# Attention kernel, one core: three quarters of the row exponentials kept instead of half, exchanged within and not across the two partition halves, V times them in 64x32 tiles, and all exchange DMAs on one queue

## Chip, cores and metric

One Trainium2 chip, one core of it. The metric is the device time of one execution in microseconds (us), lower is better. The kernel before has a median of 650.43 us over three runs (650.21 to 651.04).

## What is computed

The input x is 8 batches of 512 tokens by 512 features, all float32. Queries, keys and values are projections of x with biases; a condition vector of each batch is projected with the same Wq and Wk and added to queries and keys. Then come attention with 16 heads of 32 features and a residual.

```python
cQ = split_heads(x @ Wq.T + bq) + split_heads(cond @ Wq.T + bq)
cK = split_heads(x @ Wk.T + bk) + split_heads(cond @ Wk.T + bk)
V = split_heads(x @ Wv.T + bv)
attn = softmax(einsum("bhqd,bhkd->bhqk", cQ, cK) / sqrt(32))
out = x + merge_heads(einsum("bhqk,bhkd->bhqd", attn, V))
```

## The kernel before

The work is cut into T = 32 groups t, each of one batch (b = t // 4) and four heads. A group has 512 query rows, worked in four blocks of 128 (qc). For each block and each head j:

- **Row scores** (row_scores, L641): a 32x128 weight tile against 512 keys. The four heads sit on four bands of 32 partitions, so that four such matmuls fill the array, each into a PSUM bank of its own.
- **Row maxima** on VectorE (one_max L593, row_max_of L650), then the **row exponential** on ScalarE with the sum of each row (denominators, L701).
- These exponentials lie with queries on the partitions, while V needs keys there. For half of the query blocks (KQ = 2 of NS = 4) they are **kept** in SBUF: VectorE turns them in 32x32 squares (turn_kept, L660, four instructions of 1024 columns a group), and DMAs exchange the off-diagonal blocks between the four bands of 32 partitions (swap_kept, L682). Six pairs of blocks, three moves each (a block to the side, its partner into its place, the side into the partner's): 18 DMAs of 128 KB a group, some issued by SP and some by GpSimd. For the other half, **the rest**, scores are made a second time with keys on the partitions (less_max L772 subtracts the maxima, scores_of_rest L785), and eight exponentials go through ScalarE again (rest_leaves, L799).
- **V** (times_v_half, L840): weight tiles of 128 partitions by 32 columns, four side by side, 32 matmuls of 256 columns for each group. Row sums (spread_sums L875) and a reciprocal (L885) follow; VectorE turns the result back (L912), GpSimd scales it and adds the residual (L913, L914), and SP stores it with four DMAs (L917).

The **projections** of the next batch run in between. Each is a Strassen-like scheme: an item is "first" or "other" of q, k or v for a half u; MADE lists them, three a group. Their matmuls (product, L462) are 128x32 tiles again. What combines the products is shared by VectorE (L487, L531, L555, L1236, L1238), ScalarE copies and GpSimd additions. x comes in 32-row bands by four DMAs a block (L172), is turned by VectorE (L372), and comes again as the residual (L190).

The order on every engine is written out by hand (manual_schedule): an engine takes its instructions in the order of the code, and waits for semaphores in that order. This holds for the DMA queues of SP and GpSimd too. The loop runs thirds(t) for t = 1 to 28, one group each; below it is called a step. Step t multiplies V for group t-1, makes the rest of group t, and the row scores and maxima of groups t+1 and t+2. A first part makes weights, condition and group 0; a last part does groups 29 to 31.

In a step TensorE switches six times between the two tile shapes: 32x128 for scores, 128x32 for V and projections. A stretch of one shape is called a burst.

## Time and profile before

| what | us |
|---|---|
| median of three runs | 650.43 |
| span of the profiled execution, first to last instruction | 648.4 |
| TensorE (PE) busy | 641.6 |
| VectorE (DVE) busy | 600.1 |
| ScalarE (ACT) busy | 533.9 |
| GpSimd (POOL) busy | 410.6 |

The profiled execution has no time of its own beside its span; the median of the runs stands 2.0 us above the span. The page gives busy time by engine and by group of instructions; the timeline shows instructions in order of time, runs of the same kind merged into one row; a row's numbers are its start and its length in us, and the length ends with the last instruction's end, so that the distance to the next row's start says better what a row costs. Matmuls come in the trace as two records each, weight loads as well. The waits view sums who waited for whom.

### The profile page before, as it was taken

The numbers are of one execution on the slowest core, as the hardware profiler recorded it, in microseconds if no ns is written. First come the engines' busy times: TensorE is split into PE (matmuls) and PEld (weight loads), VectorE is DVE, ScalarE is ACT, GpSimd is POOL, SyncE is SP. The second block draws the span as 40 slices with busy tenths as digits, with TensorE's granted clock in tenths as the row PEclk, the third lists the DMA queues.
The fourth block names the chain that finished last, engine by engine and source line by source line (L and its number), as shares of the span: only waits on it lengthen the run. The fifth ranks groups of instructions, "written<-read, shape, count | busy, mean of one in ns | idle before, by whom it ended". The sixth has DMA issues, their size and how long they took to land. (4 is left out here: it accounts for less than half of the span.)

```text
span 648.4 us, 24814 instructions
## 1 busy us (share of the span) xinstructions
PE 641.6 (99%) x9856; PEld 356.7 (55%) x9856; DVE 600.1 (93%) x845; ACT 533.9 (82%) x1364; POOL 410.6 (63%) x651
## 2 busy tenths in 40 slices
PE   9999999999999999999999999999999999999997
PEld 8445555556555555555555555555555555555531
DVE  3799999999999999999999999999999999999887
ACT  2479888889888989888888988898988888898564
POOL 3633655686665776758567776558766576665650
PEclk9999999999999999999999999999999999999999
DMA  7615688878888788977888978788888767797921
GB/s 191 107 27 84 131 164 172 168 169 191 168 171 174 158 182 177 200 156 153 181 178 170 201 154 186 161 175 169 179 193 162 153 144 164 153 188 155 199 48 34
DMA packets 248457, 102.02 MB, mean 157 GB/s; under 512 B 229962, under 2 KB 230474, under 8 KB 248340
## 3 DMA queue, kind: packets, MB, share of 16 engines
q1 hardware_dynamic: 234196, 65.54, 53.6%
q0 software_dynamic: 12384, 33.83, 20.2%
q8 instruction: 78, 1.28, 0.8%
q10 hardware_dynamic: 1760, 1.05, 0.5%
q14 instruction: 39, 0.32, 0.1%
HBM read 19.75 MB, written 8.39 MB: 43 GB/s over the span
## 5 line engine op out<-in xcount | busy, mean ns | idle before, releaser
L593 DVE TENSOR_REDUCE nmax<-psum 128x1 f32<-128x512 f32 x279 | 177.5, 675 | 9.3 <-PE psum L641 4.9
L701 ACT ACTIVATE psum<-psum,nmax 128x512 f32<-128x512 f32 x248 | 165.3, 678 | 3.6 <-DVE nmax L593 3.0
L641 PE MATMUL psum<-kT,qT 32*128 32x512 f32 x1024 | 162.0, 612 | 0.0
L701 ACT ACTIVATE store<-psum,nmax 128x512 f32<-128x512 f32 x204 | 139.6, 701 | 24.9 <-DVE nmax L593 24.7
L682 POOL DMA_DIRECT2D store<-store x258 | 129.0, 504 | 48.9 <-DMA store<-store 31.8
L799 ACT ACTIVATE store<-psum 128x512 f32<-128x512 f32 x232 | 119.8, 602 | 33.2 <-PE psum L785 33.2
L660 DVE STREAM_TRANSPOSE store<-store 128x1024 f32<-128x1024 f32 x116 | 138.9, 1217 | 0.0
L650 DVE TENSOR_REDUCE nmax<-psum 128x2 f32<-128x1024 f32 x98 | 118.8, 1212 | 0.0
L840 PE MATMUL psum<-store,v 128*32 128x256 f32 x1856 | 106.8, 381 | 0.9 <-DMA store<-store 0.9
L840 PEld LDWEIGHTS psum<-store,v 128*32 128x32 f32 x1856 | 57.2, 110 | 57.9 <-ACT wT_q L632 21.2
L913 POOL TENSOR_TENSOR res<-res,recs 128x512 f32<-128x512 f32 x30 | 31.4, 1046 | 89.0 <-DVE res L912 89.0
L785 PE MATMUL psum<-qT,kT 32*128 32x256 f32 x928 | 83.8, 374 | 0.0
L641 PEld LDWEIGHTS psum<-kT,qT 32*128 32x128 f32 x1024 | 61.5, 183 | 35.4 <-issue 17.8
L785 PEld LDWEIGHTS psum<-qT,kT 32*128 32x128 f32 x928 | 60.8, 184 | 5.9 <-issue 0.3
L701 ACT ACTIVATION_READ_ACCUMULATOR psum<-psum,nmax 128x1 f32 x248 | 55.0, 222 | 0.0
L203 POOL TENSOR_TENSOR xr<-xr,bvs 128x512 f32<-128x512 f32 x30 | 38.6, 1285 | 16.4 <-DMA xr<-in_x_dram 15.7
L462 PE MATMUL psum<-wc_v,xc 128*32 128x256 f32 x768 | 47.7, 379 | 0.0
L462 PE MATMUL psum<-xc,wc_q 128*32 128x256 f32 x720 | 44.7, 379 | 0.0
L462 PE MATMUL psum<-xc,wc_k 128*32 128x256 f32 x720 | 44.5, 379 | 0.0
L701 ACT ACTIVATION_READ_ACCUMULATOR store<-psum,nmax 128x1 f32 x204 | 44.3, 217 | 0.0
L914 POOL TENSOR_TENSOR res<-res,xr 128x512 f32<-128x512 f32 x30 | 38.3, 1278 | 2.3
L462 PE MATMUL psum<-xT,wT_k 128*32 128x256 f32 x480 | 34.5, 382 | 0.0
(191 smaller groups left out, 972.4 us busy)
## 6 DMA issues: line engine op xcount, KB each, us to landing
store<-store SPq DMA_DIRECT2D x264, 128.0 KB, 2.7
store<-store POOLq DMA_DIRECT2D x258, 128.0 KB, 3.8
out_dram<-res SPq DMA_DIRECT2D x122, 64.0 KB, 3.7
xr<-in_x_dram SPq DMA_DIRECT2D x120, 64.0 KB, 4.2
x<-in_x_dram SPq DMA_DIRECT2D x112, 64.0 KB, 3.3
w_q<-in_L_cond_Wq_dram SPq DMA_DIRECT2D x4, 256.0 KB, 3.9
w_v<-in_L_cond_Wv_dram SPq DMA_DIRECT2D x16, 64.0 KB, 2.5
w_k<-in_L_cond_Wk_dram SPq DMA_DIRECT2D x16, 48.0 KB, 2.7
```

The source lines that it names most:

```text
L203: nc.gpsimd.tensor_tensor(xr[t], xr[t], bias, ALU.add)
L462: nc.tensor.matmul(pt[r], still[:, r], moving, start=(kc == kcs[0]), stop=(kc == kcs[-1]))
L593: nc.vector.tensor_reduce(nmax[t][:, qc, j : j + 1, 0], pt, AX.X, ALU.max, negate=True)
L641: nc.tensor.matmul(pt, qkT["q", t][r, qc * P : (qc + 1) * P], qkT["k", t][r, :], start=True, stop=True,)
L650: nc.vector.tensor_reduce(nmax[t][:, qc, pr * 2 : pr * 2 + 2, 0], pt, AX.X, ALU.max, negate=True)
L660: nc.vector.transpose(e, e)
L682: (nc.gpsimd if here else nc.sync).dma_start(to, of)
L701: nc.scalar.activation(to, of, AF.Exp, bias=nmax[t][:, qc, j, :], accum_out=sums[t][:, qc, j, :],)
L785: nc.tensor.matmul(banks(j)[:, i * HS : (i + 1) * HS], qkT["k", t][r, kc * P : (kc + 1) * P], qkT["q", t][r, KQ * P :], start=False, stop= ...
L799: nc.scalar.activation(e[:, j], banks(j), AF.Exp)
L840: nc.tensor.matmul(pt[j * HD : (j + 1) * HD, half * HS : (half + 1) * HS], vs[b % 2][:, kc, (g * HG + j) * HD : (g * HG + j + 1) * HD], e, ...
L914: nc.gpsimd.tensor_tensor(y, y, xr.pop(t), ALU.add)
```

## The change

- KQ is 3: of four query blocks three are kept, one is the rest. The kept buffer of a group is half as large again; two groups alternate in it.
- The exchange is no longer between four bands of 32 partitions but within each half of 64: in a half h, block(0) (partitions 0-31 of the half) and block(1) (32-63) change places through a side buffer in the opposite half. Two parts (query blocks 0 and 1 together, block 2 alone), three moves, two halves: 12 DMAs a group, six of 256 KB and six of 128 KB, all issued by SP.
- After that, each half of 64 partitions holds the keys of one parity, and V is multiplied in tiles of 64 partitions by 32 columns, eight of them filling the array; the two halves add into two banks (lo, hi). Keys that lie in the other half need V rows from there: cross_v copies V into crossed_v with four more DMAs a batch, on SP.
- The rest is one block: its scores are 128 columns wide, its subtraction of maxima one instruction for each head, its exponentials four.
- Item sums: VectorE no longer takes part. ScalarE copies both banks out (with the biases), GpSimd does all additions.
- Row maxima are all taken bank by bank (16 a step). VectorE turns six kept pieces a step, and the result in three pieces.
- The banks of PSUM go round by a list (take, give). The order of a step is written anew: four bursts of scores (blocks 2; 3; rest and 0; 1), and between them an item with V on the rest, V on the kept part, an item, an item.
- Before the loop, blocks 3, 0 and 1 of group 1 are made (before: all four, and block 0 of group 2), and one item more. After the loop, block 2 of group 29, all four of group 30 and block 0 of group 31 are left (before: 1, 2 and 3 of group 30, and block 0 of group 31). Step 28 has two items.

SP, from the middle of the loop; "store<-store" are the exchange, "maxT" the transposing DMA of the split maxima (turn_max), "res" the results, DMAHW and DMASW the semaphores that tell of landings of SP's and GpSimd's DMAs. Before:

```order
L727 DMA_TRANSPOSE maxT_3615<-split 128x4x128 [waits DMAHW0_49,PE_49,Pool_49]
L682 DMA store<-store 32x1024 [waits DMASW4_49,DMAHW1_49,DVE_49,Activation_49]
L682 DMA store<-store 32x1024 [waits DMAHW2_49,DMASW5_49]
L190 DMA xr_3724<-in_x_dram 32x16x32 [waits DMAHW3_49]
L190 DMA xr_3724<-in_x_dram 32x16x32 [waits DMAHW4_49]
L190 DMA xr_3724<-in_x_dram 32x16x32 [waits DMAHW5_49]
L190 DMA xr_3724<-in_x_dram 32x16x32 [waits DMAHW6_49]
L682 DMA store<-store 32x1024 [waits DMAHW7_49,DMAHW1_49]
L682 DMA store<-store 32x1024 [waits DMAHW2_49,DMAHW0_49]
L682 DMA store<-store 32x1024 [waits DMASW2_49]
```

SP, the same place of a step, after the change:

```order
L678 DMA store<-store 32x2048 [waits DMAHW3_49,DVE_49]
L678 DMA store<-store 32x2048 [waits DMAHW4_49]
L678 DMA store<-store 32x2048 [waits DMAHW5_49,DMAHW3_49,PE_49]
L678 DMA store<-store 32x2048 [waits DMAHW6_49,DMAHW4_49,PE_49]
L725 DMA_TRANSPOSE maxT_3651<-split 128x1x128 [waits DMAHW7_49,PE_49,Pool_49]
L678 DMA store<-store 32x2048 [waits DMAHW5_49,DMAHW0_49]
L678 DMA store<-store 32x2048 [waits DMAHW6_49,DMAHW1_49]
L678 DMA store<-store 32x1024 [waits DMAHW2_49,DVE_49,Activation_49]
```

Before, SP issued its first moves, then loads, and then the second moves, and the third moves stood on GpSimd's queue. Now the second move of each half stands directly behind the first moves and waits for their landing (DMAHW3 and DMAHW4 are the semaphores of the first two rows), and the third moves follow on the same queue behind the second.

TensorE, the rows around V. Before, with all of V in one burst beside sums and items:

```order
L462 MATMUL psum<-xT,wT_k 32x256 x4
L641 MATMUL psum<-kT_2087,qT_1953 128x512 x8
L840 MATMUL psum<-store,v_164 32x256 x32
L875 MATMUL psum<-apart_2589,modulo 32x16 x4
L462 MATMUL psum<-wT_v,xT 32x256 x8
```

TensorE, the same place after the change:

```order
L820 MATMUL psum<-store,v_164 32x128 x16
L872 MATMUL psum<-apart_2698,modulo 32x16 x4
L642 MATMUL psum<-kT_2224,qT_1965 128x512 x4
L837 MATMUL psum<-store,v_164 32x192 x32
L837 MATMUL psum<-store 32x192 x32
L772 LDWEIGHTS onesb
```

V on the rest (L820) stays beside the sums and an item; V on the kept part (L837) is 64 matmuls of 192 columns and stands alone between two bursts of scores.

```diff
-    KQ = NS // 2
+    KQ = NS - 1
+    R = KQ * P
...
     def room(t):
-        at = (t + 1) % 3 * 4
-        return store[:, at : at + 4].rearrange("p g c (h s) -> p g c h s", s=P)
+        at = t % 2 * 6
+        return store[:, at : at + 6].rearrange("p c i s -> p (c i s)").rearrange(
+            "p (g q j x e) -> p g q j x e", g=2, q=KQ, j=HG, e=BL
+        )
...
+    def item(b, n, u, kind, at):
...
+            def multiply():
+                product(n, b, u, 1, one_[:, 0])
+                product(n, b, u, 7, one_[:, 1])
+                if n == "v":
+                    product(n, b, u, 6, two_[:, 0])
+                else:
+                    product(n, b, u, 6, two_[:, 1])
+                    product(n, b, u, 2, two_[:, 0], (0,))
+            def sums():
+                add(c12, c12, c2[:, 0, :], ALU.add)
+                add(c22, c22, c12, ALU.add)
+                if n != "v":
+                    add(c1[:, 0, :], c1[:, 0, :], c2[:, 0, :], ALU.add)
...
+            def multiply():
+                product(n, b, u, 4, one_[:, 0])
+                product(n, b, u, 5, one_[:, 1])
+                product(n, b, u, 2, two_[:, 0], (0, 1) if n == "v" else (1,))
+                product(n, b, u, 3, two_[:, 1])
...
+            def sums():
+                two = c12.rearrange("p (u s) -> p u s", u=2)
+                add(two, m45[:, 1], two, ALU.add)
+                if n == "v":
+                    v = vs[b % 2].rearrange("p k (h f) -> p (k h) f", h=2)
+                    add(quarters(c1), m23, quarters(v[:, u * 2 + 1 : u * 2 + 5 : 3, :]), ALU.add)
+                    add(quarters(c2), m45, quarters(twice(c22)), ALU.add)
+                else:
+                    add(quarters(c2), m45, quarters(twice(c22)), ALU.add)
...
-    def turn_kept(t, n):
-        pr = slice(n % NP * 2, n % NP * 2 + 2)
-        e = kept[t][:, :, n // NP, pr, :].rearrange("p g h s -> p g (h s)")
-        nc.vector.transpose(e, e)
-    APART = [(a, g) for a in range(HG) for g in range(a + 1, HG)]
-    between = store[:, 16:18]
-    def swap_kept(t, move, some=range(6)):
-        later = 6 if t % 4 == 1 else 2
-        def part(a, g):
-            return kept[t][a * BL : (a + 1) * BL, g].rearrange("p c h s -> p (c h s)")
-        for n in some:
-            a, g = APART[n]
-            at = (n + 2) % HG * BL
-            aside = (store[:, 6:8] if t == KEPT[-1] else between)[at : at + BL, n // HG]
-            aside = aside.rearrange("p i s -> p (i s)")
-            to, of = [(aside, part(a, g)), (part(a, g), part(g, a)), (part(g, a), aside)][move]
-            if t < KEPT[-1]:
-                here = move == 2 or move == 0 and n >= later
-            else:
-                here = move > 0 and n >= 3
-            (nc.gpsimd if here else nc.sync).dma_start(to, of)
...
+    def turn_kept(t, qc, prs=range(NP)):
+        for pr in prs:
+            e = kept[t][:, :, qc, pr * 2 : pr * 2 + 2].rearrange("p g j x e -> p g (j x e)")
+            nc.vector.transpose(e, e)
+    between = store[:, 14:16].rearrange("p c i s -> p (c i s)")
+    def swap_kept(t, move, part):
+        qs = slice(0, 2) if part == 0 else slice(2, KQ)
+        w = (qs.stop - qs.start) * HG * HS
+        for h in range(2):
+            def block(a):
+                e = kept[t][h * 64 + a * BL : h * 64 + (a + 1) * BL, 1 - a, qs]
+                return e.rearrange("p q j x e -> p (q j x e)")
+            at = (1 - h) * 64 + part * BL
+            side = between[at : at + BL, :w]
+            to, of = [(side, block(0)), (block(0), block(1)), (block(1), side)][move]
+            nc.sync.dma_start(to, of)
...
+    rest_of = store[:, 12:14].rearrange("p c i s -> p (c i) s")
+    def scores_of_rest(t, bs):
...
-                maxT[t][r, KQ * P :].unsqueeze(1).broadcast_to([3, 2, HS]),
+                maxT[t][r, R:].unsqueeze(1).broadcast_to([3, NS, P]),
...
+        for kc in range(NS):
+            for j in range(HG):
+                r = slice(j * HD, (j + 1) * HD)
+                nc.tensor.matmul(
+                    psum[:, bs[j], kc * P : (kc + 1) * P],
+                    qkT["k", t][r, kc * P : (kc + 1) * P],
+                    qkT["q", t][r, R:],
+                    start=False,
+                    stop=(kc == NS - 1),
+                )
+    def rest_leaves(bs):
+        for j in range(HG):
+            nc.scalar.activation(rest_of[:, j], psum[:, bs[j], :], AF.Exp)
...
+    crossed_v = store[:, 16:18].rearrange("p c i s -> p (c i s)").rearrange(
+        "p (c d) -> p c d", c=NS
+    )
+    def cross_v(b, u):
+        for h in range(2):
+            to = crossed_v[(1 - h) * 64 : (2 - h) * 64, u::2]
+            nc.sync.dma_start(to, vs[b % 2][h * 64 : (h + 1) * 64, u::2])
+    def times_v_rest(t, bank):
...
+    def times_v_kept(t, lo, hi):
+        b, g = divmod(t, G)
+        of = [(x, c) for x in range(2) for c in (0, 2, 1, 3)]
+        for x, c in of:
+            v = crossed_v if x else vs[b % 2]
+            for j in range(HG):
+                for h in range(2):
+                    half = slice(h * 64, (h + 1) * 64)
+                    nc.tensor.matmul(
+                        psum[j * HD : (j + 1) * HD, (lo, hi)[h], : R // 2],
+                        v[half, c, (g * HG + j) * HD : (g * HG + j + 1) * HD],
+                        kept[t][half, :, :, j, c * 2 + (h ^ x), :].rearrange("p a q e -> p q a e"),
+                        start=((x, c) == of[0]),
+                        stop=((x, c) == of[-1]),
+                    )
...
+    def third(t):
+        if t % G == 1 and t > 1:
+            cross_v(t // G, 1)
+        k3 = take(HG)
+        rows(t, 2, k3)
+        maxima(t, 2, k3)
+        row_exponentials(t, 2, k3)
+        give(*k3)
+        turn_kept(t, 1)
+        swap_kept(t, 0, 0)
+        swap_kept(t, 1, 0)
...
+    def step(t):
+        b, r = divmod(t, G)
+        third(t)
+        at = take(2)
+        multiply, leave, sums_of = item(*next(made), at)
+        multiply()
+        hi, pd = rest_and_sums(t - 1)
+        leave(0)
+        leave(1)
+        rec = reciprocals(t - 1, pd)
+        give(*at, pd)
+        aparts[t] = masked(t)
+        sums_of()
+        if r == 0:
+            combine_x(b + 1, 0, nc.gpsimd)
+        n = take(HG)
+        rows(t + 1, KQ, n)
+        maxima(t + 1, KQ, n)
+        row_exponentials(t + 1, KQ, n)
+        split_max(t + 1)
+        turn_max(t + 1)
+        if t - 1 in KEPT:
+            lo = take(1)
+            y = kept_leaves(t - 1, lo[0], hi)
         else:
...
+            lo = []
+            y = turned(t - 1, hi)
+        give(*n[:3], *lo, hi, n[3])
+        swap_kept(t, 2, 0)
+        finish(t - 1, y, rec)
+        turn_kept(t, 2)
+        if t == 1:
+            turn_next()
+        swap_kept(t, 0, 1)
+        put(t - 1, y)
+        if r == 0:
+            cross_v(b, 0)
+        s = take(HG)
+        scores_of_rest(t, s)
+        rest_leaves(s)
+        give(*s)
+        k1 = take(HG)
+        rows(t + 1, 0, k1)
+        maxima(t + 1, 0, k1)
+        swap_kept(t, 1, 1)
+        swap_kept(t, 2, 1)
+        if t > 1:
+            bias_residual(t)
+        at = take(2)
+        multiply, leave, sums_of = item(*next(made), at)
+        multiply()
+        row_exponentials(t + 1, 0, k1, (0, 1))
+        leave(0)
+        row_exponentials(t + 1, 0, k1, (2, 3))
+        leave(1)
+        give(k1[0], k1[1], at[0], k1[2], k1[3], at[1])
+        turn_next()
+        if r == 0:
+            combine_x(b + 1, 1, nc.gpsimd)
+        sums_of()
+        k2 = take(HG)
+        rows(t + 1, 1, k2)
+        maxima(t + 1, 1, k2)
+        row_exponentials(t + 1, 1, k2)
+        give(*k2)
+        turn_kept(t + 1, 0)
+        more = next(made, None)
+        if more:
+            at = take(2)
+            multiply, leave, sums_of = item(*more, at)
+            multiply()
+            leave(0)
+            leave(1)
+            sums_of()
+            give(*at)
+        load_blocks()
+        load_residual(t + 1)
     for t in KEPT[:-1]:
...
+        step(t)
...
+    def more_maxima(t, qc):
+        n = take(HG)
+        rows(t, qc, n)
+        maxima(t, qc, n)
+        return n
+    n = more_maxima(t + 1, 0)
+    lo = take(1)[0]
+    y = kept_leaves(t - 1, lo, hi)
+    give(*n, lo, hi)
+    swap_kept(t, 2, 0)
+    finish(t - 1, y, rec)
+    turn_kept(t, 2)
+    swap_kept(t, 0, 1)
+    put(t - 1, y)
+    s = take(HG)
+    scores_of_rest(t, s)
+    rest_leaves(s)
+    give(*s)
+    give(*more_maxima(t + 1, 1))
+    swap_kept(t, 1, 1)
+    swap_kept(t, 2, 1)
+    late.append(store[:, :4].rearrange("p c i s -> p (c i) s"))
+    give(*more_maxima(t + 1, 2))
+    hi, pd = rest_and_sums(t)
+    rec = reciprocals(t, pd)
+    give(pd)
+    give(*more_maxima(t + 1, 3))
+    lo = take(1)[0]
+    y = kept_leaves(t, lo, hi)
+    finish(t, y, rec)
+    put(t, y)
+    n = more_maxima(t + 2, 0)
```

543 lines of the change are left out of this document (153 added, 390 removed), and 4 rows, old and new, of the table TURNS.

## The prediction

> **What bounds the kernel now.** First the page's busy times, then the same for 27 steps of the loop (us: PE, PEld, DVE, ACT, POOL busy with their instructions, clock, DMA share, GB/s).
>
> ```profile
> PE 641.6 (99%) x9856; PEld 356.7 (55%) x9856; DVE 600.1 (93%) x845; ACT 533.9 (82%) x1364; POOL 410.6 (63%) x651
> ```
> ```profile
> 87.20:604.50 517.30, 517.29 (x8428) 294.00 (x8432) 495.16 (x673) 450.75 (x1168) 354.65 (x580) 1.00 0.82 171
> ```
>
> PE is never without a matmul, at the full clock; DVE is busy 96% of the loop; the DMA engines stand at a share of 0.82. The timeline of DVE gives the length of a step and the price of each of its operations.
>
> ```profile
> 72.67 0.24 DVE L885 RECIPROCAL recs<-psum 128x16 f32<-128x16 f32 x1
> 72.83 0.66 DVE L912 STREAM_TRANSPOSE res<-psum 128x512 f32<-128x512 f32 x1
> 73.41 2.32 DVE L660 STREAM_TRANSPOSE store<-store 128x1024 f32<-128x1024 f32 x2
> 75.65 0.67 DVE L372 STREAM_TRANSPOSE xT<-x 128x512 f32<-128x512 f32 x1
> 76.25 1.27 DVE L593 TENSOR_REDUCE nmax<-psum 128x1 f32<-128x512 f32 x2
> 77.43 1.21 DVE L650 TENSOR_REDUCE nmax<-psum 128x2 f32<-128x1024 f32 x1
> ...
> 589.96 0.66 DVE L912 STREAM_TRANSPOSE res<-psum 128x512 f32<-128x512 f32 x1
> ```
>
> L912 turns one result a step: 72.83 in step 1, 589.96 in step 28. So 27 steps take 517.13 us, **19.15 us a step**. Now PE over the second half of a step:
>
> ```profile
> 309.96 0.39 PE L772 MATMUL psum<-maxT,onesb 3*128 3x512 bf16 x4
> 310.19 1.03 PE L785 MATMUL psum<-qT,kT 32*128 32x256 f32 x16
> 311.06 1.02 PE L641 MATMUL psum<-kT,qT 32*128 32x512 f32 x8
> 312.01 1.07 PE L462 MATMUL psum<-xT,wT_k 128*32 128x256 f32 x16
> 312.90 1.91 PE L462 MATMUL psum<-xc,wc_k 128*32 128x256 f32 x32
> 314.63 0.61 PE L462 MATMUL psum<-xT,wT_k 128*32 128x256 f32 x8
> 315.17 2.07 PE L641 MATMUL psum<-kT,qT 32*128 32x512 f32 x16
> 317.18 3.66 PE L840 MATMUL psum<-store,v 128*32 128x256 f32 x64
> 320.65 0.23 PE L875 MATMUL psum<-apart,modulo 128*32 128x16 f32 x8
> ```
>
> V's 64 records of 256 columns fill 317.18 to 320.65: 3.47 us, 0.217 us for four side by side. The 56 records of an item's burst (312.01 to 315.17) would take 3.03 us at that rate and take 3.16: **a change of tile shape costs about 0.13 us**. Starts follow each other at this rate through the whole step: PE sets the pace. But SP, which issues DMAs, has no room either:
>
> ```profile
> 299.39 2.72 SPq L682 DMA_DIRECT2D store<-store  x4
> 302.17 3.13 SPq L190 DMA_DIRECT2D xr<-in_x_dram  x4
> 305.34 3.68 SPq L682 DMA_DIRECT2D store<-store  x6
> 309.13 4.35 SPq L917 DMA_DIRECT2D out_dram<-res  x4
> 313.53 2.64 SPq L172 DMA_DIRECT2D x<-in_x_dram  x4
> 316.28 1.22 SPq L727 DMA_TRANSPOSE maxT<-split  x1
> 317.68 1.18 SPq L682 DMA_DIRECT2D store<-store  x2
> 318.91 4.41 SPq L190 DMA_DIRECT2D xr<-in_x_dram  x4
> ...
> 327.83 2.30 SPq L917 DMA_DIRECT2D out_dram<-res  x4
> 330.18 4.78 SPq L172 DMA_DIRECT2D x<-in_x_dram  x4
> ```
>
> Each row begins within 0.2 us of the end of the one before. A free issue costs 0.59 us (327.83 to 330.18: 2.35 us for four). Several take longer, 1.09 us each at 309.13, as if the way behind them were full. Six exchanges in a row take 3.79 us (305.34 to 309.13), 0.63 us for each 128 KB or 207 GB/s. That SP has kept up needed GpSimd's second queue:
>
> ```profile
> L682 POOL DMA_DIRECT2D store<-store x258 | 129.0, 504 | 48.9 <-DMA store<-store 31.8
> ```
> ```profile
> store<-store SPq DMA_DIRECT2D x264, 128.0 KB, 2.7
> ```
> ```profile
> DMA to landing us min/median/max: 2.2/3.5/6.3
> ```
> ```profile
> POOL store L682 <- DMA store<-store: 31.8, 30, 2.4
> ```
> ```profile
> SPq L682 <- DMA store<-store: 2.4, 5, 0.9
> ```
>
> An exchange lands 2.7 us after its issue on SP (median), 2.2 at the least on either queue. Waits for such landings cost GpSimd 31.8 us in the run, and SP 2.4.
>
> **The change, part by part, for one step.**
>
> *PE.* The rest's scores are 32 records of 128 columns, not 256: half of twice (311.06 - 310.19), so 0.87 us less; four subtractions of maxima go (310.19 - 309.96), 0.23 less. V on the rest, 32 records of 128 columns, costs a quarter of 3.47, 0.87 us. V on the kept part is 128 records of 192 columns in 64x32 tiles, a shape that no row shows. If eight run at once, as four do of the shapes that fill the array, it is 16 rounds of 0.163 (0.217 x 192/256): 2.60 us, and V together is as dear as before. If only four did, 5.2 us; below 2.60 nothing points, since in both known shapes a full array gives 0.217. I take 2.60. Six changes of shape become eight, +0.26 us. Projections keep their matmuls. Sum: 19.15 - 1.10 + 0.26 = **18.3 us**.
>
> The trace's 0.13 us at each change of shape is what the Trainium skill names in TensorEngine Tiling (Array Packing), Key Properties: changing the tiling mode drains the array. Its list of configurations has 64x32 with eight tiles, which would mean 2.60 us; no row here can test that, and it stays open by the bounds above.
>
> *DVE.* 16 maxima x 0.59 (77.43 - 76.25 for two) = 9.4; six kept pieces x 1.12 (75.65 - 73.41 for two) = 6.7; the result in three pieces, 0.58 (73.41 - 72.83) and about 0.05 for each cut more, 0.7; reciprocal 0.16, x 0.6. Sum 17.6 us, against 18.3 now (495.16 / 27). It fits under PE, with little room.
>
> *ACT and POOL.*
>
> ```profile
> L799 ACT ACTIVATE store<-psum 128x512 f32<-128x512 f32 x232 | 119.8, 602 | 33.2 <-PE psum L785 33.2
> ```
> ```profile
> L541 POOL TENSOR_TENSOR qT<-qT 128x256 f32<-128x256 f32 x14 | 10.3, 735 | 0.0
> L1240 POOL TENSOR_TENSOR v<-aside,v 128x512 f32<-128x512 f32 x14 | 17.9, 1278 | 12.5 <-DVE v L1238 12.5
> ```
>
> ACT loses four exponentials (2.4 us) and gains some three copies of that size, near 16 of its 16.7 us (450.75 / 27). POOL loses 9.2 issues of 0.50 (4.6) and has, for three items, 5.5 additions of 256 columns and three of 512: 4.0 + 3.8 us, of which it did about half before. From 13.1 us (354.65 / 27) it stays under 15. Neither is the bound; the slack that hides them is more than 2 us.
>
> *SP.* It issues 12 exchanges, 12 loads and stores, one transposing DMA, one V copy on average. With 0.63 for an exchange, 0.59 for others and 1.22 for the transposing one, that alone is 16.5 us. To this come the landings that the queue order now waits for. Let a 128 KB exchange land 2.2 us after its issue at the least, 256 KB 2.85 (0.63 more). Part 0 from its first issue: first moves at 0 and 0.6; the second move of half 0 at 2.85; half 1's data comes behind half 0's, lands at 4.1, its second move goes then; third moves at 5.7 and 6.95, the transposing DMA between; done 7.55. Part 1's first moves, to 8.8. Stores to 11.1. Second moves to 12.4; the third waits for a landing 2.7 us after 11.1 (median, since it stands behind stores) and is done at 15.0. Eight loads to 19.6, V copies 0.6: **20.2 us**. With the least landing everywhere it is 19.7; with the median everywhere 21.2; if the halves didn't queue behind each other, 0.6 less than the least, 19.1. I take 20.2, since in part 0 each pair is alone in the queue.
>
> The partitions bear on the last case. The trace's 207 GB/s for exchanges of 32 partitions agrees with the Trainium skill, SBUF — State Buffer, Door 1: 32 partitions reach 8 of 16 ports, an estimate of 218 GB/s by its figures, and partitions 64 up use the other eight. By that rule the two halves would not share ports, and 20.2 would become 19.6 and the time 670 us; by the queue's order they share engines. The sum goes by the rows.
>
> What waits for SP: V on the kept part of group t-1 needs part 1's third move, and stands in PE's order ahead of all of a step's later bursts. So the step is the longest of the four, 20.2 us, and the loop 28 x (20.2 - 19.15) = **+29 us**.
>
> *Ahead of the loop and behind.* Ahead: one item more (3.16), two bursts of row scores less (0.95 each, 312.01 - 311.06): +1.3. Behind, DVE:
>
> ```profile
> 603.57 1.89 DVE L593 TENSOR_REDUCE nmax<-psum 128x1 f32<-128x512 f32 x3 [0.30 <-PE psum L641]
> ...
> 616.95 1.25 DVE L1322 TENSOR_REDUCE nmax<-psum 128x1 f32<-128x512 f32 x2
> ```
>
> From the loop's end to group 30 takes 13.4 us now. It gets two more sets of maxima (4.7) and four kept pieces (4.5), and saves some 3.5 us of V and copies that are spread behind it: +5.7. Sum +7 us; between +3 and +12, as the missing item of step 28 or the last exchange decides.
>
> 648.4 + 29 + 7 = 684.4 us for the profiled execution, **686.5** with the 2.0 us by which the median stands above it.
>
> **Rivals.**
>
> - *SP keeps up, PE's saving stays.* The exchanges finish within 18.3 us, if landings fall where SP would have waited anyway. For it: SP's issues alone are 16.5 us, and its slow ones may have been slowed by GpSimd's queue, which is now empty. Against: two waits for landings in a row, in each step. It decides below an SP cycle of 18.9 (648.4 - 28 x 0.25 + 7 is the time before). At 18.3 to 18.7 a step and +6: 631 to 642, with 2.0 **638** us.
> - *PE and DVE hand over too tightly.* DVE has 17.6 of 18.3 us, each bank is reused as soon as it is left. A step of 18.8 to 19.2 gives 646 to 657, about **653** us. For it: 96% of DVE now; against: PE waits for DVE hardly ever now.
> - *64x32 tiles run four at a time.* PE's step becomes 18.3 + 2.6 = 20.9, longer than SP's: 648.4 + 49 + 6 + 2, **705** us. Against it: both shapes in the trace fill the array.
>
> **How the numbers follow.** Chances: SP bounds 0.55, SP keeps up 0.20, hand-over 0.15, four tiles 0.10. A measurement of this kernel tells apart about 0.2% (649.1 to 651.7). Hand-over gives 0.03 faster, 0.05 within, 0.07 slower; so faster 0.23, within 0.05, slower 0.72. SP's bounds of 19.1 to 21.2 a step give 656 to 715. The range 640 to 715 takes these, hand-over, and the upper end of "keeps up"; about 2 in 10 lie outside.
>
> **What the profile after would show.** If I am right: PE idle before V on the kept part, released by an exchange DMA, 1 to 2 us a step; L894's starts 20 us apart; SP's second and third moves waiting for store<-store. L837 at 163 ns a round of eight confirms PE's part, 326 refutes it. Steps near 18.3 us, with SP idle in front of DVE's turns, would refute the SP sum.

## The result and the profile after

The changed kernel takes 781.43 us (median of 4 runs, 777.06 to 782.4) against 650.54 us for the kernel before (4 runs): a ratio of 1.200, interval 1.197 to 1.203. The forecast was slower, 686.5 us, with a range up to 715; the sign holds, the size doesn't. The profiled execution took 782.4 us with a span of 780.6, so 132.2 us more than the span before.

First the page's busy times of the changed kernel, then four steps of its loop, one row each (us; busy time with instructions of PE, PEld, DVE, ACT, POOL; granted clock; DMA share; GB/s).

```profile
PE 688.8 (88%) x12524; PEld 397.8 (51%) x12524; DVE 592.5 (76%) x913; ACT 510.8 (65%) x1310; POOL 418.3 (54%) x537
```
```profile
285.90:305.20 19.30, 19.30 (x420) 11.48 (x412) 18.32 (x28) 16.61 (x44) 13.34 (x17) 1.00 0.73 148
305.20:325.70 20.50, 19.07 (x407) 11.20 (x400) 17.57 (x28) 15.66 (x43) 11.48 (x16) 1.00 0.72 147
325.70:349.60 23.90, 21.58 (x420) 13.38 (x416) 18.42 (x28) 16.71 (x45) 18.17 (x21) 0.93 0.70 146
349.60:380.70 31.10, 23.10 (x405) 13.23 (x401) 17.68 (x28) 15.65 (x43) 11.44 (x16) 0.78 0.69 152
```

DVE, ACT and POOL have about as much to do as before. PE is busy 47 us more, some of it at half clock, and has idle time, which it did not have; its granted clock is 0.931 over the run, 0.998 before. Steps come in fours, one batch: 19.3, 20.5, 23.9 and 31.1 us. Over the loop the product that spreads the row sums (L875 before, L872 after) marks the step; here its first and its 28th record in the timeline of PE, before and then after.

```profile
71.47 0.23 PE L875 MATMUL psum<-apart,modulo 128*32 128x16 f32 x8
...
588.64 0.23 PE L875 MATMUL psum<-apart,modulo 128*32 128x16 f32 x8
```
```profile
75.89 0.23 PE L872 MATMUL psum<-apart,modulo 128*32 128x16 f32 x8
...
696.75 0.23 PE L872 MATMUL psum<-apart,modulo 128*32 128x16 f32 x8
```

So 27 steps take 620.86 us instead of 517.17: **23.0 us a step instead of 19.15**, +103.7. Ahead of the first mark there are 4.4 us more, behind the last 83.85 instead of 59.76, +24.1. Together 132.2.

What PE waits for, SP's waits, and how long an exchange is under way, from the waits and the DMA part of the changed kernel (waits: us in total, times, longest; DMA: issues, KB, us from issue to landing, median):

```profile
PE psum L837 <- DMA store<-store: 39.8, 13, 6.3
...
PE psum L837 <- DMA store<-v: 23.4, 7, 4.9
```
```profile
SPq L678 <- DMA store<-store: 155.7, 123, 3.6
```
```profile
store<-store SPq DMA_DIRECT2D x174, 256.0 KB, 3.4
store<-store SPq DMA_DIRECT2D x174, 128.0 KB, 3.0
store<-v SPq DMA_DIRECT2D x32, 256.0 KB, 3.8
```

SP waited 2.4 us for landings of exchanges in the whole run before, and waits 155.7 us now. V on the kept part (L837) is where PE waits, for an exchange or for a copy of V. SP's timeline over a step without a copy of V (311.57 to 333.76) and a step with copies (to 360.45):

```profile
311.57 6.66 SPq L678 DMA_DIRECT2D store<-store  x4
318.34 1.19 SPq L725 DMA_TRANSPOSE maxT<-split  x1
319.62 2.90 SPq L678 DMA_DIRECT2D store<-store  x4
322.57 2.31 SPq L908 DMA_DIRECT2D out_dram<-res  x4
324.99 3.42 SPq L678 DMA_DIRECT2D store<-store  x4
328.50 2.18 SPq L167 DMA_DIRECT2D x<-in_x_dram  x4
330.73 2.93 SPq L185 DMA_DIRECT2D xr<-in_x_dram  x4
333.76 6.26 SPq L678 DMA_DIRECT2D store<-store  x4
...
346.99 1.35 SPq L813 DMA_DIRECT2D store<-v  x2
348.39 6.12 SPq L678 DMA_DIRECT2D store<-store  x4
...
359.00 1.34 SPq L813 DMA_DIRECT2D store<-v  x2
360.45 6.02 SPq L678 DMA_DIRECT2D store<-store  x4
```

A row whose four issues take 6.66 us holds waits inside: issues alone are 2.4. Each row begins as the one before ends. From 74.3 to 700.2 us (27 of SP's cycles) its own records give 16.0 us of issues a step, 1.4 us between issues, and 5.5 us in front of an exchange that waits for another one's landing. That is 22.9 of the cycle's 23.2.

And PE, from the wait of the step without copies to the end of V in the next:

```profile
329.75 2.31 PE L837 MATMUL psum<-store,v 64*32 64x192 f32 x57 [2.32 <-ACT psum L690]
...
334.65 0.39 PE L772 MATMUL psum<-maxT,onesb 3*128 3x512 bf16 x4
334.88 1.06 PE L782 MATMUL psum<-qT,kT 32*128 32x128 f32 x32
...
349.77 1.14 PE L642 MATMUL psum<-kT,qT 32*128 32x512 f32 x8
355.83 3.01 PE L837 MATMUL psum<-store,v 64*32 64x192 f32 x57 [4.91 <-DMA store<-store]
...
363.52 1.53 PE L837 MATMUL psum<-store 64*32 64x192 f32 x32 [3.08 <-DMA store<-v]
...
365.39 1.92 PE L782 MATMUL psum<-qT,kT 32*128 32x128 f32 x32
```

PE stands still for 2.32 us, a step later for 4.91 us, and then for 3.08 in the middle of V. (The first of these is put down to ScalarE, whose exponential ended at 329.56; part 1's third move landed in its first half at 329.51 and in its second at 330.12, for which V stands again inside its row, and in e15, where there is no exchange, V waits for no such exponential.) L782's 32 records take 1.92 us behind the long waits, 1.06 otherwise. The trace's clock records put PE at half clock for 106 us up to 750 us, in pieces of 3.4 us and multiples of it, each right behind such a wait. The Trainium skill states this in TensorE: Matmul & The Clock Gate, Part 1 (The HAM clock gate): about 3.4 us of idle time halves the clock, and as much work brings it back. The trace agrees on the length of the pieces, not on what starts one: here 2.3 us of waiting (329.75) were enough, with half clock from 330.9 to 334.4 us.

### The profile page after: what moved, and what is told of

It reads as the page before. It is cut to its first block, busy times and chain, and to the rows that moved or that the text cites. A ratio compares the mean times of both kernels' runs of the same rounds, so it can differ in the third digit from the quotient of the medians.

```text
span 780.6 us, 29911 instructions
## 1 busy us (share of the span) xinstructions
PE 688.8 (88%) x12524; PEld 397.8 (51%) x12524; DVE 592.5 (76%) x913; ACT 510.8 (65%) x1310; POOL 418.3 (54%) x537
## 5 line engine op out<-in xcount | busy, mean ns | idle before, releaser
L615 DVE TENSOR_REDUCE nmax<-psum 128x1 f32<-128x512 f32 x498 | 305.5, 674 | 32.9 <-PE psum L642 32.7
L690 ACT ACTIVATE store<-psum,nmax 128x512 f32<-128x512 f32 x348 | 235.7, 692 | 41.1 <-DVE nmax L615 40.6
L661 DVE STREAM_TRANSPOSE store<-store 128x1024 f32<-128x1024 f32 x174 | 204.2, 1212 | 0.0
L792 ACT ACTIVATE store<-psum 128x512 f32<-128x512 f32 x116 | 59.9, 604 | 137.6 <-PE psum L782 137.6
L837 PE MATMUL psum<-store,v 64*32 64x192 f32 x1856 | 69.0, 397 | 57.1 <-DMA store<-store 39.8
L894 DVE STREAM_TRANSPOSE res<-psum 128x192 f32<-128x192 f32 x58 | 18.9, 363 | 130.1 <-issue 111.5
L690 ACT ACTIVATE psum<-psum,nmax 128x512 f32<-128x512 f32 x132 | 87.1, 660 | 32.3 <-DVE nmax L615 31.6
L837 PEld LDWEIGHTS psum<-store,v 64*32 64x32 f32 x1856 | 44.5, 126 | 91.0 <-issue 39.8
L837 PE MATMUL psum<-store 64*32 64x192 f32 x1856 | 67.3, 388 | 24.3 <-DMA store<-v 23.4
L837 PEld LDWEIGHTS psum<-store 64*32 64x32 f32 x1856 | 50.1, 127 | 31.5 <-DMA store<-v 27.2
L782 PEld LDWEIGHTS psum<-qT,kT 32*128 32x128 f32 x928 | 38.2, 220 | 4.3 <-issue 3.3
L782 PE MATMUL psum<-qT,kT 32*128 32x128 f32 x928 | 38.4, 307 | 0.9 <-issue 0.8
```

The source lines that it names most:

```text
L615: nc.vector.tensor_reduce(nmax[t][:, qc, j : j + 1, 0], pt, AX.X, ALU.max, negate=True)
L661: nc.vector.transpose(e, e)
L690: nc.scalar.activation(to, of, AF.Exp, bias=nmax[t][:, qc, j, :], accum_out=sums[t][:, qc, j, :],)
L782: nc.tensor.matmul(psum[:, bs[j], kc * P : (kc + 1) * P], qkT["k", t][r, kc * P : (kc + 1) * P], qkT["q", t][r, R:], start=False, stop=(kc ...
L792: nc.scalar.activation(rest_of[:, j], psum[:, bs[j], :], AF.Exp)
L837: nc.tensor.matmul(psum[j * HD : (j + 1) * HD, (lo, hi)[h], : R // 2], v[half, c, (g * HG + j) * HD : (g * HG + j + 1) * HD], kept[t][half ...
```

## Experiments

The first theory was the **queue**: SP's in-order queue is occupied without a gap and its cycle is the step. Its **rivals** were the row of landings by itself (the chain), the copies of V, half clock on PE, and the bytes in the DMA engines. After eight runs another came up, **the loop**, told at e9. Each variant ran once, beside a run of the kernel before (650.0 to 650.4 us); the changed kernel's own runs scatter by 0.7%, and smaller differences from it are not read. Times are device times; the spans are 1.8 to 2.1 us shorter (e16: 3.0).

**e1, third moves by GpSimd.**

```diff
-            nc.sync.dma_start(to, of)
+            (nc.gpsimd if move == 2 else nc.sync).dma_start(to, of)
```

> Edit: the third move of each exchange (four DMAs a step) is issued by GpSimd instead of SP. Queue theory: in the changed kernel SP is never idle except for landings of its own exchanges, and its cycle of 23.2 us a step (16.0 issuing, 1.4 between issues, 5.5 waiting for landings) sets the step. Four issues (2.4 us) and about half of the waits (2.7) leave SP, its cycle falls to some 18, PE's own 18.8 us a step takes over: 650 to 675 us, granted clock near 1.00. Chain theory: what costs is the row of landings from the first to the third move of part 1, on whichever queue; it is as long as before: 740 us or more. Clock theory (PE at half clock after waits is the loss): follows the waits, so no number of its own here.

Measured: 817.17 us, slower still. The waits:

```profile
POOL store L678 <- DMA store<-store: 186.4, 43, 9.0
...
PEld psum L459 <- POOL xc L389: 73.3, 6, 13.2
```

The wait for the second move went along into GpSimd's order, and its other work (the result's products, the sums of x, L389) stood behind it. So the run tells of the new wait. It decides neither on the queue theory nor on the chain theory, whose 740 us or more it meets.

**e2, copies of V left out after the first batch.**

```diff
-        if t % G == 1 and t > 1:
-            cross_v(t // G, 1)
...
-        if r == 0:
-            cross_v(b, 0)
```

> Edit: the copies of V into the other half of the partitions are made for the first batch only (leaves out the copies of the seven later batches, whose V on the kept part then reads old rows). V-copy theory: the steps of 24 and 31 us are those around a copy; without it all steps are like the other two, 19.4 to 20.5 us: 28 x (19.9 - 23.3) = -95, about 685 us. Queue theory: a copy lengthens SP's cycle from 22.5 to 26.5-28.8 us once in four steps, so without it the cycle is some 22.3 us in every step and the sum falls by 28 x 1.0 to 1.3: 745 to 755 us.

Measured: 745.51 us, the queue theory's number. The steps of 24 and 31 us were not the copies' doing alone: the steps are now nearly all between 20 and 25 us, and the short ones are gone too.

**e3, PE kept busy in the wait.**

```diff
             lo = take(1)
+            for i in range(12):
+                for j in range(HG):
+                    r = slice(j * HD, (j + 1) * HD)
+                    nc.tensor.matmul(psum[r, lo[0], :HS], wc["q"][:, 0, 0, r], wc["q"][:, 0, 1, :],
+                                     start=True, stop=True)
```

> Edit: 48 further matmuls of 256 columns (2.6 us at full clock) on constant operands into the bank that V on the kept part is about to overwrite, ahead of it in PE's order, so that PE is busy in part of the wait. Clock theory: the loop of the changed kernel has 106 us at half clock, which costs PE some 45 us; with shorter idle times the clock stays up and the time falls to 735-750 us although PE has 73 us more work. Queue theory: SP's cycle sets the step and PE has 4 us of room in it, so the time stays within 1.5% of 781, whatever the clock does. If neither, and PE's length counts in full: 781 + 73 = 854 us.

Measured: 809.67 us at a clock of 0.992. The edit was mis-sized and not clean. Its timeline:

```profile
316.30 5.39 PE L1169 MATMUL psum<-wc_q 128*32 128x256 f32 x96
```

An f32 product is two records, so 48 are 96 records and 5.3 us; 18.8 + 5.3 is the 24.1 us a step that it took, with PE as the bound. And the added `r` hid the step's own `r`, which left out the first copies of V and half of the combined blocks of x for later batches. e13 does it properly.

**e4, loads between part 0's first and second moves.**

```diff
         swap_kept(t, 0, 0)
+        if t > 1:
+            load_blocks()
+            load_residual(t)
         swap_kept(t, 1, 0)
...
-        load_blocks()
-        load_residual(t + 1)
```

> Edit: the loads of x and of the residual (up to eight DMAs a step) go into SP's queue between the first and the second moves of part 0 instead of at the step's end; nothing else moves. Queue theory: SP waits there some 4 us for two landings while it has 4.5 us of loads to issue; the loads cover it, the cycle falls from 23.2 to 19.2-19.8 us: 670 to 690 us. Rival (the DMA engines are what is full: the loads' packets then delay the exchanges by as much as they cover): 760 us or more.

Measured: 765.51 us, the rival's side. SP's timeline:

```profile
304.50 2.92 SPq L167 DMA_DIRECT2D x<-in_x_dram  x4
307.47 3.02 SPq L185 DMA_DIRECT2D xr<-in_x_dram  x4
310.58 1.15 SPq L678 DMA_DIRECT2D store<-store  x2
```

The wait ahead of the second moves (310.58) is covered, but then a move takes longer to land, as the chain of waits has it:

```profile
311.22 4.35 DMA store<-store
```

Whichever move stands directly behind the eight loads lands late. In the changed kernel these are part 0's first moves, 3.9 and 4.3 us from issue to landing in the two halves, with 3.1 and 3.5 for the second moves; here they are the second moves, 4.1 and 3.8, with 3.3 and 3.9 for the first (medians over the groups). Part 1's first move is issued 12.9 us after part 0's, not 9.3 (medians). The exchange got longer by most of what the rest of the queue got shorter.

**e5, no loads from the fifth group and batch on.**

```diff
+            if 4 < t < T - 3:
+                xr[t] = shared[0]
+                return
...
+        if n >= 4 * NC:
+            xs[n] = xs[4 * NC - 2 + n % 2]
```

> Edit: from the fifth group on no residual is loaded and from the fifth batch on no x (leaves them out: later groups add an old residual, later batches are made from old x). Queue theory, as the first runs leave it (SP is occupied without a gap: issues, 45 ns between them, and landings that it waits for): eight issues of 0.55 us go from most steps, the cycle falls from 23.2 to some 18.7 us, PE's own 18.8 us takes over except around the copies of V: 665 to 690 us. Rival (the row of landings from part 0's first move to part 1's third sets the step by itself, whatever else SP issues): 720 us or more.

Measured: 714.78 us, above the queue theory's 665 to 690 and just below the rival's 720. SP's waits:

```profile
SPq L685 <- DVE recs L889: 38.4, 18, 4.1
```

L685 is here the exchange. SP is no longer occupied throughout: part 0's first moves wait for DVE. Something else closes at 20.7 us a step.

**e6, residual and later copies of V issued by ScalarE.**

```diff
-                nc.sync.dma_start(xr[t][h...
+                (nc.scalar if 1 < t < T - 2 else nc.sync).dma_start(xr[t][h...
...
-            nc.sync.dma_start(to, vs[b % 2][h...
+            (nc.scalar if b else nc.sync).dma_start(to, vs[b % 2][h...
```

> Edit: the residual's loads (four a step) and the copies of V in the loop (four in four steps) are issued by ScalarE; nothing else moves, the same bytes. Queue theory: SP loses 4 x 0.58 and 0.7 us a step, its cycle falls to 20.1: 690 to 700 us; ScalarE rises from 16 to 19 us, so up to 715. Rival (the bytes in the DMA engines, not the issues): 750 us or more.

Measured: 764.42 us, on the rival's side. But SP lost issues and gained waits:

```profile
SPq L908 <- DMA xr<-in_x_dram: 29.7, 11, 4.0
```

Its stores now wait for loads of the residual, which ScalarE issues late in its own order. It isn't the data that they wait for: nearly all of these stores wait on the very semaphore that they raise themselves. SP's and ScalarE's DMAs take the same eight landing semaphores in turn, and the load that had this one last has not landed. So the run tells of this new wait, and leaves open whether issues or bytes cost.

**e7, third moves by GpSimd, late in its order.**

```diff
-        swap_kept(t, 2, 0)
         finish(t - 1, y, rec)
+        swap_kept(t, 2, 0)
...
-        swap_kept(t, 2, 1)
...
         sums_of()
+        swap_kept(t, 2, 1)
         k2 = take(HG)
```

> Edit: the third moves by GpSimd as in e1, but later in its order: part 0's behind the products and sums of the result, part 1's behind the projection sums of the step's second item. In e1 GpSimd stood 186 us waiting for second moves to land, with the result's products queued behind. If that in-order wait was what made e1 slow, and SP's occupied time is the bound otherwise: SP falls to some 18.2 us, 655 to 680 us. If the chain of landings sets the step, on whichever queue: 740 us or more.

Measured: 742.22 us, the best that still computes everything, and just past the 740 of the chain of landings.

```profile
POOL store L678 <- DMA store<-store: 71.9, 34, 5.0
```

GpSimd's wait is 71.9 us instead of e1's 186.4: its place in the order was most of e1. But the third move is issued later than SP could, and the step is 21.5 us.

**e8, e7 with e4.**

> Edit: e7 and e4 together: third moves by GpSimd late in its order, loads between part 0's first and second moves. Queue theory: SP has 14 us of issues a step and no landing of part 0 to stand for, PE's own 18.8 us sets the step: 648 to 662 us. Rival (loads in front of an exchange's second move delay it in the DMA engines, as e4's landings of 4.4 and 5 us suggest, and the next step waits for it): 690 us or more.

Measured: 777.3 us, the rival. SP's waits:

```profile
SPq L678 <- DVE recs L882: 95.0, 21, 6.3
```

SP now waits for DVE most, in front of first moves, so its queue is not the bound; V still waits for the exchange.

**The loop, and e9.** Take E from part 0's first issue for a group to the start of V on its kept part, V for that product, A from its end to the first issue two groups on (two groups are under way at a time). E + V + A is two steps. In the changed kernel the rows at 311.57, 329.75, 334.65 and 360.45 us above give E 18.2, V 4.9, A 25.8. The means over groups 3 to 26, from the same records:

| run | us | E | V | A | half of the sum |
|---|---|---|---|---|---|
| changed kernel | 781.4 | 20.3 | 5.2 | 21.0 | 23.3 |
| e2 no copies of V | 745.5 | 18.6 | 4.3 | 20.7 | 21.8 |
| e4 loads inside | 765.5 | 23.2 | 4.5 | 17.7 | 22.7 |
| e5 no loads | 714.8 | 20.1 | 3.8 | 17.2 | 20.5 |
| e6 ScalarE issues | 764.4 | 21.8 | 4.4 | 18.7 | 22.4 |
| e7 GpSimd late | 742.2 | 21.3 | 4.3 | 17.4 | 21.5 |
| e8 e7 and e4 | 777.3 | 24.6 | 4.4 | 16.8 | 22.9 |
| e9 no loads, no copies | 691.6 | 19.6 | 3.2 | 16.5 | 19.6 |
| e11 part 1 first | 775.8 | 19.8 | 5.3 | 20.7 | 22.9 |
| e12 e11, ScalarE loads | 805.3 | 24.1 | 3.0 | 20.7 | 23.9 |
| e13 PE kept busy | 797.6 | 22.5 | 4.7 | 20.2 | 23.7 |
| e14 half the bytes | 739.7 | 20.3 | 4.7 | 18.4 | 21.7 |

That the sum is the step holds by definition; where it moves is what the table tells. A, which holds rows, maxima, exponentials and turns of two groups on in PE's and DVE's order, falls from 21.0 to between 16.5 and 17.7 in e4, e5, e7, e8 and e9, and hardly at all in e2, e11 and e12. Where it falls, E does not fall by as much, and in e4, e7 and e8 it rises.

e9 is e2 and e5 together.

> Edit: e2 and e5 together (leaves out the loads of x and residual and the later copies of V). Loop theory, formed after eight runs: over two steps the time is E + V + A, with E from part 0's first issue to the start of V on the kept part (20.3 us in the changed kernel, 17.1 in its best step), V that multiplication (5.2 for 2.8 of work, because of half clock and of waits inside), A from its end to the first issue two groups on (21.0 in the changed kernel, 15.8 to 16.3 where SP is free). Here E 18.4, V 3.0, A 16.3: 18.9 us a step, no more than PE's own 18.8: 652 to 668 us. Rival (SP's occupied time plus some cost of loads and copies by themselves): the two savings add, 781 - 36 - 66 = 679 us or more.

Measured: 691.57 us, past the rival's 679. A and V came out as expected (16.5, 3.2); E is 19.6, not 18.4, and the loop theory's number had left out the time behind the loop, where the exchange stands bare. SP's waits:

```profile
SPq L685 <- DVE recs L889: 53.7, 19, 5.6
```

SP still stands for landings (132.6 us in the run), but part 0's first moves wait for DVE 2.0 us a step: SP's queue has room. PE is busy 97% between 150 and 600 us (437.26 of 450), and its granted clock is 0.982. So here PE's own work is most of the step. The loop theory is right about A; what E would be was no better foreseen than in the prediction.

**e10, e3 with 20 products**, with the same hidden `r`, so it tells nothing apart.

> Edit: as e3, but 20 extra products on constants (40 records, 2.2 us a step at full clock) instead of 48 (which were 96 records and 5.3 us, so that PE's 24.1 us set e3's step), into columns that nothing else uses. PE has 18.8 + 2.2 = 21.0 us of work a step. If half clock after waits lengthens the loop (V on the kept part takes 5.2 us for 2.8 of work, 2.4 too much, and what follows it runs slow): granted clock over 0.97 and 735 to 765 us, though PE has 62 us more work. If half clock is only a sign of the wait and SP's occupied time sets the step: 775 to 790 us. If PE's work counts in full: 840 us.

Measured: 774.96 us, with part of the copies of V left out.

**e11, part 1 ahead.** Part 0's third move by GpSimd behind `finish`, `cross_v(b, 0)` behind `swap_kept(t, 2, 1)`.

```diff
-        swap_kept(t, 2, 0)
         finish(t - 1, y, rec)
         turn_kept(t, 2)
         swap_kept(t, 0, 1)
+        swap_kept(t, 2, 0)
         put(t - 1, y)
-        if r == 0:
-            cross_v(b, 0)
```

> Edit: part 0's third move is issued by GpSimd, behind the result's products; part 1's first move follows on SP at once; the first copy of V goes behind part 1's third move instead of ahead of its second. Same bytes, same waits for data. Loop theory: part 1's chain starts 2 us sooner, E 17.4 to 18.5 and SP's cycle 20.5 to 21.2 us: 700 to 720 us. Rival (GpSimd's in-order wait again, as in e1): 760 us or more.

Measured: 775.83 us, on the rival's side and hardly less than the changed kernel. E fell by half a microsecond only, and the copies, now later, are what PE waits for:

```profile
PE psum L837 <- DMA store<-v: 43.2, 13, 6.9
```

**e12, e11 with the residual by ScalarE behind the exponentials of the rest.**

> Edit: e11, and the residual's loads issued by ScalarE right behind the exponentials of the rest (in e6 they stood at the step's end, and GpSimd waited for them). SP's cycle is then some 18.2 us, ScalarE has 18.4, the loop (18.0 + 3.0 + 16.5) / 2 = 18.8, PE 18.8: 655 to 680 us if nothing else comes in; if the loads' packets lengthen E as in e4 and e6 (by 1.5 to 2.6 us): 700 to 730 us.

Measured: 805.32 us, above both.

```profile
DVE nmax L615 <- PE psum L642: 147.9, 122, 4.5
```

ScalarE's exponentials stood in its order behind the loads that it issues (38.4 us of its waits end with a residual's landing), PE's row scores behind the exponentials, DVE's maxima behind the row scores. It is e1 over again, on ScalarE.

**e13, PE kept busy, clean:** e3 with 5 instead of 12, `part` for `r`, and columns that nothing else uses.

> Edit: 40 extra records on constants (2.2 us a step at full clock) ahead of V on the kept part, and nothing else (in e3 and e10 a loop variable of the edit hid the step's own one, so the first copies of V and half of the weight-free sums of x were left out as well). PE has 21.0 us of work a step. Clock as a cause (V on the kept part takes 5.2 us for 2.8 of work): granted clock over 0.96 and 740 to 770 us. Clock as a sign, the exchange's chain sets the step: 775 to 795 us. PE's work in full on top: 840 us.

Measured: 797.57 us at a clock of 0.957 (0.931 without): 62 us more work on PE cost 15 us, and less half clock (71 us instead of 110 in the span) brought no gain. That speaks for half clock as a sign of the wait, most of it hidden behind the loop's other legs; as the same records are also more work, the run does not price half clock by itself.

**e14, half the bytes.**

```diff
-            nc.sync.dma_start(to, of)
+            nc.sync.dma_start(to[:, : w // 2], of[:, : w // 2])
```

> Edit: each of the twelve exchange DMAs of a step moves the first half of its columns (leaves the other half unexchanged): same issues, same waits, half the bytes. If landings are long because of bytes (256 KB take 1.2 us of all sixteen engines at the 207 GB/s of the trace before), each of six landings in E is 0.3 to 0.6 us shorter and E falls by 2.5 us, SP's cycle by as much: 705 to 730 us. If a landing is a fixed time after its issue: 765 us or more.

Measured: 739.73 us, between the two. Landings in its DMA part:

```profile
store<-store SPq DMA_DIRECT2D x174, 128.0 KB, 2.3
store<-store SPq DMA_DIRECT2D x174, 64.0 KB, 2.0
```

Half the bytes took 1.1 and 1.0 us off a landing; some 2 us stay.

**e15, no exchange from group 2 on.**

```diff
     def swap_kept(t, move, part):
+        if t > 1:
+            return
```

> Edit: no exchange from group 2 on (leaves it out: V is multiplied with unexchanged rows). If the exchange is the whole of the loss, PE's own 18.8 us sets the step and the tail loses its 25 us: 643 to 656 us, granted clock near 1.00, no wait ahead of V on the kept part. If something else of the change also stands in the way (hand-over of PSUM banks between PE, DVE and ScalarE, GpSimd's sums): 670 us or more.

Measured: 665.48 us at a clock of 0.994, below the "something else" bound and above the "whole of the loss" one. The marks of its steps on PE:

```profile
75.29 0.23 PE L875 MATMUL psum<-apart,modulo 128*32 128x16 f32 x8
...
593.74 0.23 PE L875 MATMUL psum<-apart,modulo 128*32 128x16 f32 x8
```

19.20 us a step (18.1 to 19.6, 18.9 in the mean, where no copy of V is waited for; 20 to 21 where one is), and behind the last mark 70.0 us, 10.2 more than before. So the exchange is 116 of the 131 us, and **without any exchange the changed kernel is still 2% slower than the kernel before**. An order of the exchange alone can't make it the faster one, so no further version was run.

**e16, the kernel before with all exchanges on SP.**

```diff
-            (nc.gpsimd if here else nc.sync).dma_start(to, of)
+            nc.sync.dma_start(to, of)
```

> The kernel before, with all its exchange DMAs on SP instead of about half of them on GpSimd. SP is occupied 19.0 of 19.15 us there and gets 9.2 issues of 0.58 us a step more: 24.3 us a step, 648 + 28 x 5.2 = 795 us or more with the landings that it then waits for. If one queue were no limit by itself: 650 to 670 us.

Measured: 724.85 us, +74.5. The direction is the queue's, the size is not. Its timeline of SP:

```profile
307.48 1.25 SPq L727 DMA_TRANSPOSE maxT<-split  x1
...
325.84 3.79 SPq L682 DMA_DIRECT2D store<-store  x6
329.74 1.24 SPq L727 DMA_TRANSPOSE maxT<-split  x1
```

22.3 us from one transposing DMA to the next, nothing but issues, and no landing is waited for, as six pieces of each move go one behind the other. Issues of loads and stores are shorter than before: in the mean over the loop 0.55 us for a store instead of 0.75, 0.59 and 0.62 for a load of the residual and of x instead of 0.80 and 0.77. That is 2.2 us a step; 24.3 had taken them at the old length. GpSimd's transfers, which are gone, may be why; no run shows that alone.

## Why the prediction was wrong in size

- **What bounds the change: right.** V on the kept part waits for part 1's third move, SP's queue has no gap, SP's second and third moves wait for `store<-store`: all as forecast, and e2 and e16 bear it out. What the prediction did not have is how close the next bound stands: in e5, e8 and e9 SP's queue had room, and the step was still 20.5, 22.9 and 19.6 us.
- **The term that failed: SP's 20.2 us a step.** It is 23.0 to 23.2. With the step from 311.57 above, against the prediction's own times: part 0's four issues end at 6.66 instead of 4.7 us, its third moves and part 1's first at 11.0 instead of 8.8, the stores at 13.3 instead of 11.1, part 1 at 16.8 instead of 15.0, the loads at 22.1 instead of 19.6. (The means over thirteen such steps are 5.8, 10.7, 13.3, 17.5 and 22.6.) The prediction let 256 KB land 2.85 us after the issue and 128 KB 2.2 to 2.7; they take 3.4 and 3.0 (median). These were the least and the median of 128 KB pieces in a kernel whose queue never stood for them. What failed most is the reason for taking the least, that in part 0 each pair is alone in the queue: the first moves stand directly behind eight loads and land after 3.9 and 4.3 us (e4). Over 28 steps the 2.8 to 3.0 us are 78 to 84 us, the copies below among them.
- **256 KB in 2.85 us** is the least that the changed kernel shows too, but by luck. The 0.63 us for 128 KB was SP's pace of issuing (a free issue is 0.59), not of the transfer: part 0's first moves, of 256 KB, are issued 0.56 us apart. So the 207 GB/s was no rate of the transfers either, and its nearness to the 218 shows nothing.
- **The copies of V**, counted at 0.6 us a step of issues, stand in front of part 1's second moves: 6.12 us for its four issues instead of 3.42, and SP's cycle is 26.7 instead of 22.2. Without them the run is 36 us shorter, not 17.
- **The upper bound of 21.2** took the median landing everywhere, and no more than that. It left out that a landing gets longer with what stands ahead of it (e4: 4.4 us), and that several engines' orders close a loop through it (e5 to e9). Taking issues off SP, which the sum says is worth its full length, gave back two thirds of it at best (e5), nearly nothing in e8, and cost time in e1 and e12.
- **Behind the loop: +5.7 was forecast, +24.1 measured** (ahead of it +1.3 and +4.4). Part of it is DVE's and PE's work, as forecast, though larger (10.2 in e15); the rest is two exchanges with no items left to work on. PE there waits 5.09 us ahead of the last V on a kept part, and runs it at half clock.
- **PE's step: 18.3 forecast, 18.9 measured** (e15 between copies). The 128 records of V on the kept part fill 287.50 to 290.27 in the timeline, 2.77 us with a change of shape: eight 64x32 tiles at once, 163 ns a round. That rival is refuted, and the Trainium skill's eight tiles (TensorEngine Tiling (Array Packing), Available Configurations) agree. The 0.6 us more fit the changes of shape: a burst of eight row scores (344.62 to 345.69) takes 1.07 us for 0.87 of work, 0.20 and not 0.13, and a step has eight changes.

```profile
287.50 1.53 PE L837 MATMUL psum<-store,v 64*32 64x192 f32 x64
288.83 1.51 PE L837 MATMUL psum<-store 64*32 64x192 f32 x64
290.27 0.40 PE L772 MATMUL psum<-maxT,onesb 3*128 3x512 bf16 x4
...
344.62 1.14 PE L642 MATMUL psum<-kT,qT 32*128 32x512 f32 x8
345.69 1.07 PE L459 MATMUL psum<-xc,wT_q 128*32 128x256 f32 x16
```

- **Two halves on separate ports** (the Trainium skill, SBUF — State Buffer, Door 1, which would have made it 670 us): the second half's second move follows 1.0 us behind the first's (median), between the 0.6 of halves that don't share and the 1.25 of halves that queue. So the whole of that gain does not show, and this kernel is no test of it: the first and third moves go from one half to a side buffer in the other or back, so that each works on partitions of both.
- **The rivals.** "SP keeps up" and "four tiles" fell. "Hand-over" is not the bound: with no exchange PE waits in the loop for copies of V and otherwise for next to nothing (e15).

Still open: how much each of the other transfers lengthens a landing. e14 shows that half of the exchange's bytes are worth about 1 us of a landing and 42 us of the run, e4 beside the changed kernel that eight loads directly ahead of a move are worth 0.4 to 1.0 us of its landing; the rest was not taken apart.

## What to carry over

Price a chain of dependent DMAs by the landing times that it will have in its own traffic, and put the upper end of the range where each landing is a microsecond longer; the least landing of a kernel that never waits for one is a lower bound. Where a wait in an in-order queue is the limit, moving an issue to another engine moves the wait into that engine's order, with all that stands behind it there (e1, e12), and where two engines share the landing semaphores, one's DMAs wait for the other's (e6). Before weighing where to put a transfer, run the kernel without it: e15 told in one run that nothing was to be gained.

## What was not expected of the hardware

- Waits of 2.3 to 6.2 us put PE at half clock for 3.4 to 13.7 us, most of it while PE was working again.
- SP's issues of loads and stores got shorter when GpSimd's transfers were gone (e16: a store 0.55 us in the mean instead of 0.75), and an exchange's landing went from 2.7 to 2.4 us (median).
- An exchange of half the size lands only about a microsecond sooner (256 KB 3.4, 128 KB 2.3, 64 KB 2.0 us): some 2 us are there at each of these sizes.
